# Nine gather buffers instead of six in the max-aggregation stage of a graph-network kernel

## The chip, the cores and the metric

One core of one Trainium2 chip. The metric is the device time of one execution in microseconds (us). Three executions of the kernel before took 3382.38, 3366.40 and 3394.16 us; the median, 3382.38, is the time before. The three lie within 0.8% of one another.

## The reference

A graph with 6250 nodes of 256 features and 100000 edges, sorted by destination. The features are normalised, clipped at zero, passed through four graph layers and added to the input:

```python
h = jnp.maximum(_layernorm(x, axis=-1), 0.0)
# layer 1: mean over the incoming edges
h = h @ W1_self + mean(h[src] by dst) @ W1_neigh + b1
# layer 2: maximum over the incoming edges
hp = relu(h @ W2_pool + b2_pool)
hmax = segment_max(hp[src], dst); hmax = where(deg > 0, hmax, 0)
h = h @ W2_self + hmax @ W2_neigh + b2
# layer 3: (sum over the incoming edges + h) / (deg + 1)
# layer 4: mean over the incoming edges, then the last dense layer
return x + h4 @ W_fc + b_fc
```

The change is in layer 2: for each of 100000 edges a row of 512 float32 numbers is fetched, and rows of one destination are reduced by maximum.

## The kernel before

Edges are put in six blocks of 52, 100, 220, 180, 130 and 100 steps (`BLOCKS`), 782 steps in all. In a block the 128 partitions hold 128 consecutive runs of edges, and step t of a partition is the t-th edge of its run. Layer 2 goes through the blocks from the last to the first.

One step is: GpSimd (POOL) issues an indirect DMA (line 1207) that gathers 128 rows of 2 KB, 256 KB in all, from `tab_p`, the table of `hp`, into one half of a buffer X of two rows per partition; VectorE (DVE) then takes the maximum with the row before it where both edges have the same destination (line 1212, one `scalar_tensor_tensor` over 128x512). The chain of maxima runs through all steps of a block. After each two steps one more DVE instruction (line 1246) folds the pair into one row, and SyncE (SP) issues a DMA that writes that row to `rows2` (line 1251). X may be filled again when this write has landed and the first maximum of the next pair, which reads X's second row as `prev`, has run.

X comes in turn from two pools of three buffers each: `xpool`, whose buffers also serve the prologue as scratch (line 478), and `xmore`, made at line 1028 for this stage. So a buffer is used again six pairs later, and at most twelve gathers are ahead of the oldest pair in use.

Between the steps the program places other work of this stage, a little at each step:

- `hub` (lines 317 to 341): one-hot tiles on ScalarE (ACT, lines 317 and 319) and DVE (`hm`, line 321), a matmul on TensorE (PE, line 327), copies on ACT, for adjacency blocks of later layers;
- `done2` (lines 1125 to 1161): for each of 49 node tiles one or two indirect gathers `tot` on POOL (line 1116), a load `th` on ACT's queue (line 1122), transposes and matmuls into `pm_prf` (lines 1135, 1140, 1143, 1146), then `prf` on DVE (line 1150), the split into three bf16 parts `r` (lines 294 to 297, ACT and DVE in turn), and a write to `tab_r` on SP (line 1156);
- `early` (line 1178): loads `ae` on SP, products `pd` on PE (line 460), sums `acc` on DVE (line 1008);
- `carry` at the end of a block: a gather `fixf` on POOL (line 1101) and its correction on DVE (line 1107);
- `node_rows`, 49-column arithmetic on DVE at the beginning of the stage (lines 926 to 993, `nr`).

Each engine works through its queue in order. The queues' order is set when the program is built, by the builder's idea of when things are ready, not strictly by the program text: lines 952 to 983 of `node_rows`, written for about steps 21 to 28, run in the trace at 1039 to 1131 us, when DVE is at about steps 50 to 100. Semaphores are placed by the builder too.

Of the kernel before, what the change touches and what calls it, by code (L numbers as in the profile page):

```python
# [9 lines left out]
F32 = mybir.dt.float32  # L10
# [10 lines left out]
P = 128  # L21
# [28 lines left out]
@with_exitstack  # L50
def kernel(ctx, tc, *aps):
    nc = tc.nc
    keep = ctx.enter_context(tc.tile_pool(name="keep", bufs=1))
    bad = keep.tile([P, 8], F32, name="bad")
    nc.vector.memset(bad, 0.0)
    flag = []

    def settle(fp, pp):

        worst = fp.tile([P, 1], F32, name="worst")  # L60
        nc.vector.tensor_reduce(worst, bad, AX.X, ALU.max)
        ones = fp.tile([P, P], F32, name="ones_f")
        nc.vector.memset(ones, 1.0)
        pw = pp.tile([P, 1], F32, name="pw_f")
        nc.tensor.matmul(pw, ones, worst, start=True, stop=True)
        odd = fp.tile([P, 1], F32, name="odd")
        nc.vector.tensor_scalar(odd, pw, 1.0, None, op0=ALU.min)
        oddI = fp.tile([P, 1], I32, name="oddI")
        nc.vector.tensor_copy(oddI, odd)
        flag.append(nc.values_load(oddI[:1, :1], min_val=0, max_val=1))  # L70

    fast_path(tc, bad, settle, *aps)
    general = flag[0]
    with tc.If(general > 0):
        general_path(tc, *aps)
# [3 lines left out]
def fast_path(  # L79
# [18 lines left out]
    FH = W1_self.shape[1]  # L98
# [129 lines left out]
    at = 0  # L228
# [76 lines left out]
    def build(d, A, keys, pool, psb, plain=True):  # L305
# [3 lines left out]
        for w in range(d * WT, (d + 1) * WT):  # L309
            hold = {}  # L310
            for k in range(k_of[w]):
# [12 lines left out]
                def run(k=k, w=w, hots=hots, hold=hold):  # L324
# [4 lines left out]
                    if k == k_of[w] - 1:  # L329
                        c = (w % WT) * WIN  # L330
                        if plain:
                            nc.vector.tensor_reduce(most[:, w : w + 1], hold[0], AX.X, ALU.max)
                        else:
# [52 lines left out]
    def sums(pool, psg, table, F, srcT, keyT, jb, h, done, deep, hub, wait=0, counts=0, todo=(), rest=0):  # L386
# [16 lines left out]
        def gather(j):  # L403
            nc.gpsimd.indirect_dma_start(  # L404
                out=ring[:, j % deep, :], out_offset=None, in_=table,
                in_offset=bass.IndirectOffsetOnAxis(ap=srcT[:, j - jb : j - jb + 1], axis=0),
            )
# [3 lines left out]
        for g in range(g_of[h][0], NG):  # L411
            pg = bank(psg, "pg", "pg", (F + counts,))
            n = min(G, T - g * G)
            for k in range(n):
                j = g * G + k
                X = ring[:, j % deep, :]
                gather(j)
                if j + ahead < T:
                    one_hot(j + ahead)
                for part in (2, 0, 1):  # L420
                    c = counts if part == 2 else 0
                    nc.tensor.matmul(  # L422
                        pg[:, : F + c], hot[j], X[:, part * F : (part + 1) * F + c],
                        start=(k == 0 and part == 2), stop=(k == n - 1 and part == 1),
# [44 lines left out]
    G2 = 2  # L469
    ahead = ctx.enter_context(tc.tile_pool(name="ahead", bufs=1))  # L470
    xpool = ctx.enter_context(tc.tile_pool(name="xrows", bufs=3))
# [19 lines left out]
    def segments():  # L491
# [15 lines left out]
        for b, tb in enumerate(BLOCKS):  # L507
# [6 lines left out]
                                    op0=ALU.is_equal)  # L514
            nc.vector.tensor_reduce(flen, eqf[:, sl_], AX.X, ALU.add)
            nc.vector.tensor_scalar(flen, flen, -1.0, None, op0=ALU.add)
# [31 lines left out]
    with ExitStack() as pro:  # L548
# [134 lines left out]
        def check_room():  # L683
# [15 lines left out]
            nc.vector.tensor_tensor(has, has, room, op=ALU.is_gt)  # L699
            nc.vector.tensor_reduce(bad[:1, 1:2], has, AX.X, ALU.max)  # L700

# [311 lines left out]
    with tc.tile_pool(name="fl2c", bufs=1) as ck, ExitStack() as late:  # L1013
# [11 lines left out]
        nc.scalar.dma_start(mkR, stash_k[:, 1, RB1:])  # L1025
        keepT = ck.tile([P, NB, P], F32, name="keepTf")
        contT = ck.tile([P, NB, P], F32, name="contTf")
        xmore = late.enter_context(tc.tile_pool(name="xrows2", bufs=3))

        def chains():  # L1030

# [93 lines left out]
        def done2(d):  # L1125
            tots, th = totals(d)
            for _ in range(4):
                yield
            hm = tots[0]
            for t in tots[1:]:  # L1130
                nc.vector.tensor_tensor(hm, hm, t, op=ALU.max)
            yield
            pt = bank(pst, "pt", "pt_hTf", (KH, P))
            for j in range(KH):
                nc.tensor.transpose(pt[:, j, :], hm[:, j * P : (j + 1) * P], ident)
            hT = wk.tile([P, KH, P], F32, name="hTf")
            nc.scalar.copy(hT, pt)
            pm = bank(psm, "pm", "pm_prf")
            for k in range(KI):
                nc.tensor.matmul(pm, th[:, k, :], usA[:, k, :], start=(k == 0), stop=False)  # L1140
            yield
            for k in range(KI):
                nc.tensor.matmul(pm, th[:, KI + k, :], usB[:, k, :], start=False, stop=False)
            yield
            for c in range(KH):
                nc.tensor.matmul(pm, hT[:, c, :], un[:, c, :], start=False, stop=(c == KH - 1))  # L1146
                if c == 1:
                    yield
            pr = wk.tile([P, FH], F32, name="prf")
            nc.vector.tensor_add(pr, pm, prow)  # L1150
            yield
            if d < H3:
                add3(d, pr)
            r3 = early_pool[0].tile([P, 3 * FH], BF16, name="r3", bufs=2 * BATCH + 1)
            parts(pr, FH, r3)
            nc.sync.dma_start(tab_r[d * P : (d + 1) * P, :], r3)
            if EARLY[0] <= d < EARLY[1]:
                ready.append((d, r3))
                if len(ready) == BATCH or d == EARLY[0]:
                    early_products()  # L1160
            yield
# [35 lines left out]
        at = 0  # L1197
        for b in reversed(range(NB)):
            tb = BLOCKS[b]
            t0 = offs[b] // P  # L1200
            prev = None
            for s0 in range(0, tb, G2):
                n = min(G2, tb - s0)
                X = (xmore if at // G2 % 2 else xpool).tile([P, G2, FH], F32, name="X2")
                for k in range(n):
                    t = t0 + s0 + k
                    nc.gpsimd.indirect_dma_start(  # L1207
                        out=X[:, k, :], out_offset=None, in_=tab_p,
                        in_offset=bass.IndirectOffsetOnAxis(ap=srcI[:, t : t + 1], axis=0),
                    )  # L1210
                    if s0 + k:
                        nc.vector.scalar_tensor_tensor(  # L1212
                            X[:, k, :], prev, same[:, t : t + 1], X[:, k, :],
                            op0=ALU.mult, op1=ALU.max,
                        )
                    prev = X[:, k, :]
                    at += 1
                    if at > 8:
                        next(steps, None)
                        if todo and next(todo[0], 0) == 0:  # L1220
                            todo.pop(0)
                    if at == MADE_AT:
                        for _ in steps:
                            pass
                        top.close()
                        early_pool.append(
                            top.enter_context(tc.tile_pool(name="early3", bufs=1)))
                    if at <= EARLY_AT:
                        hub.advance(math.ceil(len(first) * max(0, at - 16) / (EARLY_AT - 16)))
                    else:  # L1230
                        hub.advance(len(first) + math.ceil(
                            len(rest) * (at - EARLY_AT) / (T - 100 - EARLY_AT)))
                    early.advance(early.done + math.ceil(early.left() / 40))
                    if s0 + k > 2 and ends and next(ends[0], 0) == 0:
                        ends.pop(0)
                        tiles += [d for d in reversed(range(NT)) if b_of[d][0] == last_b]
                    if tiles and not ends and begun2 < NT * (at - FIRST_AT) / (T - 20 - FIRST_AT):
                        now.append(done2(tiles.pop(0)))
                        begun2 += 1
                    for g in list(now):  # L1240
                        if next(g, 0) == 0:
                            now.remove(g)
                r0 = s0 // 2
                if s0 + n < tb:
                    t = t0 + s0 + 1
                    nc.vector.scalar_tensor_tensor(  # L1246
                        X[:, 0, :], prev, same[:, t : t + 1], X[:, 0, :],
                        op0=ALU.mult, op1=ALU.max,
                    )
                    n = 1  # L1250
                nc.sync.dma_start(
                    runs[b][r0 * P : (r0 + n) * P, :].rearrange("(g p) f -> p g f", p=P),
                    X[:, :n, :],
                )
            end = carry(b, prev)
            next(end)
            ends.append(end)
            last_b = b
# [46 lines left out]
    with ExitStack() as on:  # L1305
# [8 lines left out]
        with tc.tile_pool(name="fl3", bufs=2) as wk:  # L1314
# [32 lines left out]
            late = ((EARLY[1], 44), (44, NT), (0, EARLY[0]))  # L1347
# [681 lines left out]
```

## Time and profile before

| What | us |
|---|---|
| median of three executions | 3382.38 |
| the profiled execution | 3393.26 |
| its span, first to last instruction | 3391.8 |
| prologue and layer 1, to the first gather of layer 2 | 0 to 957 |
| layer 2, first gather to the end of the last maximum | 957 to 2330.5 |
| layer 2's end: last carry, last node tile, first loads of layer 3 | 2330.5 to 2362 |
| layers 3 and 4 | 2362 to 3391.8 |

The profiled execution is 10.9 us (0.3%) above the median. Everything that the change touches lies in the 1373 us of the second stage. A view of that stage is read by engine: busy time is what the engine computes or issues; "idle before" is what it stood still, by what ended the wait. "issue" means that the wait was for nothing that the profile shows; "remote" stands for a release whose origin is not in the trace.

### The profile page before, as it was taken

The numbers are of one execution on the slowest core, as the hardware profiler recorded it, in microseconds if no ns is written. First come the engines' busy times: TensorE is split into PE (matmuls) and PEld (weight loads), VectorE is DVE, ScalarE is ACT, GpSimd is POOL, SyncE is SP. The second block draws the span as 40 slices with busy tenths as digits, with TensorE's granted clock in tenths as the row PEclk, the third lists the DMA queues.
The fourth block names the chain that finished last, engine by engine and source line by source line (L and its number), as shares of the span: only waits on it lengthen the run. The fifth ranks groups of instructions, "written<-read, shape, count | busy, mean of one in ns | idle before, by whom it ended". The sixth has DMA issues, their size and how long they took to land.

```text
span 3391.8 us, 42009 instructions
## 1 busy us (share of the span) xinstructions
PE 2546.3 (75%) x12637; PEld 1418.2 (42%) x12719; DVE 2109.1 (62%) x5394; ACT 987.3 (29%) x2703; POOL 2098.4 (62%) x2255
## 2 busy tenths in 40 slices
PE   4557788888867565586888864873888888788888
PEld 2134455555543222233333332431333333577776
DVE  7845555555358887787878786875456656333333
ACT  4745555554146777531301110000000001000000
POOL 4265565555556687776776666664566666566664
PEclk9678999999999677798899986985999999899999
DMA  5454555555578788898988888886999998766775
GB/s 173 152 142 137 158 165 168 162 169 169 170 247 267 260 281 264 282 303 272 297 295 279 270 292 265 271 262 202 344 328 340 350 331 306 242 198 199 200 204 167
DMA packets 354555, 812.52 MB, mean 240 GB/s; under 512 B 58078, under 2 KB 151494, under 8 KB 354284
## 3 DMA queue, kind: packets, MB, share of 16 engines
q0 software_dynamic: 146080, 513.65, 49.5%
q1 hardware_dynamic: 150152, 240.63, 19.6%
q10 hardware_dynamic: 58084, 55.44, 5.5%
q8 instruction: 103, 1.69, 0.2%
q14 instruction: 136, 1.11, 0.1%
HBM read 611.14 MB, written 199.17 MB: 239 GB/s over the span
## 4 chain that ended last, share of the span: by engine, by line
PE 46%; DMA 15%; issue 14%; DVE 13%; another core or an unknown queue 4%; POOL 3%; ACT 3%; SPq 0%; ACTq 0%; DVEq 0%; POOLq 0%
PE pd L460 19%; PE pg L422 12%; DVE X L1212 6%; DMA X<-rows,srcIf 5%; DMA ring<-tab_r,srcE 4%; PE pm_hp L896 3%; PE pb L327 3%; PE pm_hp L899 2%; POOL X L1207 2%; DVE X L1246 2%; PE pm_prf L1146 1%; DMA zt<-tab_r 1%; DMA rows<-X 1%; PE pm_w L261 1%
## 5 line engine op out<-in xcount | busy, mean ns | idle before, releaser
L1207 POOL DMA_INDIRECT X<-rows,srcIf x782 | 894.8, 1144 | 406.8 <-issue 195.2
L422 PE MATMUL pg<-ring,hot 128*128 128x256 bf16 (+2 forms) x3375 | 689.4, 315 | 132.6 <-DMA ring<-tab_r,srcE 47.4
L404 POOL DMA_INDIRECT ring<-tab_h,srcT x474 | 450.8, 951 | 330.0 <-issue 94.7
L460 PE MATMUL pd<-zt,ac 128*128 128x256 bf16 (+1 forms) x3442 | 584.4, 300 | 59.6 <-issue 41.8
L422 PEld LDWEIGHTS <-hot 128*128 128x128 bf16 x3390 | 337.9, 101 | 401.5 <-issue 246.1
L404 POOL DMA_INDIRECT ring<-tab_r,srcE x342 | 330.9, 967 | 203.5 <-PE pg L422 99.7
L460 PE MATMUL pd<-r,ae 128*128 128x512 bf16 x1493 | 376.0, 398 | 98.3 <-DVE acc L1008 49.1
L460 PEld LDWEIGHTS <-ac 128*128 128x128 fp8e4 x3462 | 338.2, 99 | 217.0 <-issue 91.8
L404 POOL DMA_INDIRECT ring<-tab_s,srcE x314 | 300.2, 956 | 192.5 <-PE pg L422 65.0
L441 DVE SCALAR_TENSOR_TENSOR acc<-pg,M,acc 128x259 f32<-128x259 f32 (+2 forms) x518 | 273.0, 560 | 234.5 <-PE pg L422 122.1
L327 PE MATMUL pb<-hm,hs 128*128 128x392 bf16 x781 | 260.7, 380 | 170.7 <-ACT A L337 64.1
L319 ACT ACTIVATE hs<-ht,onef 128x128 bf16<-128x128 bf16 x781 | 290.8, 398 | 299.8 <-PE pb L327 173.9
L1212 DVE SCALAR_TENSOR_TENSOR X<-X,samef 128x512 f32<-128x512 f32 x391 | 291.9, 747 | 67.4 <-DMA X<-rows,srcIf 48.1
L400 DVE TENSOR_SCALAR hot<-iota_bf,keyE 128x128 bf16<-128x128 bf16 x656 | 156.2, 268 | 279.2 <-PE pg L422 180.9
L1212 DVE SCALAR_TENSOR_TENSOR X<-X,samef,X 128x512 f32<-128x512 f32 x385 | 286.8, 745 | 33.7 <-DMA X<-rows,srcIf 25.8
L460 PEld LDWEIGHTS <-ae 128*128 128x128 fp8e4 x1536 | 155.9, 101 | 332.2 <-issue 191.5
L1246 DVE SCALAR_TENSOR_TENSOR X<-X,samef 128x512 f32<-128x512 f32 x385 | 287.2, 746 | 4.8 <-DVE nr L966 0.4
L400 DVE TENSOR_SCALAR hot<-iota_bf,keyT 128x128 bf16<-128x128 bf16 x474 | 119.6, 266 | 173.2 <-PE pg L422 65.8
L1146 PE MATMUL pm_prf<-unf,hTf 128*128 128x512 f32 x392 | 200.1, 645 | 17.3 <-issue 10.2
L460 PE MATMUL pd<-Z,A 128*128 128x256 bf16 (+1 forms) x1176 | 193.9, 281 | 6.4 <-issue 6.0
L327 PEld LDWEIGHTS <-hs 128*128 128x128 bf16 x781 | 81.1, 105 | 251.7 <-issue 140.1
L896 PE MATMUL pm_hp<-Wa,th 128*128 128x512 f32 x196 | 118.6, 736 | 83.6 <-ACT th L890 43.7
(314 smaller groups left out, 3076.5 us busy)
## 6 DMA issues: line engine op xcount, KB each, us to landing
rows<-X SPq DMA_DIRECT2D x385, 256.0 KB
tab_r<-r SPq DMA_DIRECT2D x49, 384.0 KB
tab_a<-A SPq DMA_DIRECT2D x18, 784.0 KB
tab_t<-th SPq DMA_DIRECT2D x49, 256.0 KB
rows<-hpf SPq DMA_DIRECT2D x49, 256.0 KB
th<-tab_t ACTq DMA_DIRECT2D x49, 256.0 KB
X<-rows,srcIf POOLq DMA_INDIRECT x782
ac<-tab_a ACTq DMA_DIRECT2D x108, 112.0 KB
```

The lines of the kernel that those rows point to most:

```text
L319: nc.scalar.activation(hots[0], t, AF.Relu, bias=one, scale=-1.0)
L327: nc.tensor.matmul(hold[0], hots[0], hots[1], start=(k == 0), stop=(k == k_of[w] - 1))
L400: nc.vector.tensor_scalar(hot[j], iota_b, keyT[:, j - jb : j - jb + 1], None, op0=ALU.is_equal)
L404: nc.gpsimd.indirect_dma_start(out=ring[:, j % deep, :], out_offset=None, in_=table, in_offset=bass.IndirectOffsetOnAxis(ap=srcT[:, j - jb ...
L422: nc.tensor.matmul(pg[:, : F + c], hot[j], X[:, part * F : (part + 1) * F + c], start=(k == 0 and part == 2), stop=(k == n - 1 and part == 1),
L441: nc.vector.scalar_tensor_tensor(acc[d], pg, m, acc[d], op0=ALU.mult, op1=ALU.add)
L460: nc.tensor.matmul(hold[0][:, : F + c], a, z[:, part * F : (part + 1) * F + c], start=(s == ss[0] and part == 2), stop=(s == ss[-1] and pa ...
L896: nc.tensor.matmul(ph, th[:, k, :], Wa[:, k, :], start=(k == 0), stop=False)
L1146: nc.tensor.matmul(pm, hT[:, c, :], un[:, c, :], start=False, stop=(c == KH - 1))
L1207: nc.gpsimd.indirect_dma_start(out=X[:, k, :], out_offset=None, in_=tab_p, in_offset=bass.IndirectOffsetOnAxis(ap=srcI[:, t : t + 1], axis=0),
L1212: nc.vector.scalar_tensor_tensor(X[:, k, :], prev, same[:, t : t + 1], X[:, k, :], op0=ALU.mult, op1=ALU.max,)
L1246: nc.vector.scalar_tensor_tensor(X[:, 0, :], prev, same[:, t : t + 1], X[:, 0, :], op0=ALU.mult, op1=ALU.max,)
```

## The change

The second pool gets six buffers, and the choice goes round nine: pairs 0, 3 and 6 of each nine take one of `xpool`'s three, the others one of `xmore`'s six.

```diff
-        xmore = late.enter_context(tc.tile_pool(name="xrows2", bufs=3))
+        xmore = late.enter_context(tc.tile_pool(name="xrows2", bufs=6))
...
-                X = (xmore if at // G2 % 2 else xpool).tile([P, G2, FH], F32, name="X2")
+                X = (xpool if at // G2 % 9 in (0, 3, 6) else xmore).tile(
+                    [P, G2, FH], F32, name="X2")
```

`at` counts steps over all blocks, `G2` is 2. A buffer has 2 x 512 x 4 = 4096 bytes per partition, so the stage holds 12 KB more, and the pools that are made after `xmore` (`fl2`, and `fw2`, later `early3` in its place) lie 12 KB higher.

## The prediction

> **What bounds the kernel now.** I read the table of costliest groups first, because it names the gather as the largest POOL group and the maxima as the largest DVE work:
>
> ```profile
> L1207 POOL DMA_INDIRECT X<-rows,srcIf x782 | 894.8, 1144 | 406.8 <-issue 195.2 <-DVE X L1212 47.5 <-DVE X L1246 39.3
> L1212 DVE SCALAR_TENSOR_TENSOR X<-X,samef 128x512 f32<-128x512 f32 x391 | 291.9, 747 | 67.4 <-DMA X<-rows,srcIf 48.1 <-issue 12.4 <-DVE X L1212 1.3
> ```
>
> 782 gathers keep POOL busy 894.8 us, and it is idle 406.8 us before them. Next the busy times of layer 2 alone, from its first gather to its last maximum:
>
> ```profile
> core 0: us, PE busy (x) PEld busy (x) DVE busy (x) ACT busy (x) POOL busy (x), PEclk, DMA share, GB/s
> 957.00:2330.00 1373.00, 960.64 (x3149) 434.86 (x3192) 1091.26 (x2061) 468.59 (x1332) 968.08 (x843) 0.83 0.86 278
> ```
>
> No engine is full: DVE 1091/1373 = 79%, POOL 968/1373 = 71%, PE 70%, DMA 0.86. The stage is a chain of queues that stop each other. So I turn to who waits for whom in the same window, POOL first:
>
> ```profile
> engine line waited for: us in total, times, longest us
> POOL X L1207 <- issue: 195.2, 623, 1.5
> POOL X L1207 <- DVE X L1212: 47.5, 37, 6.5
> POOL X L1207 <- DVE X L1246: 39.3, 35, 5.3
> POOL X L1207 <- DMA rows<-hpf: 33.2, 1, 33.2
> ...
> POOL X L1207 <- DVE hm L321: 19.6, 17, 6.0
> POOL X L1207 <- DMA rows<-X: 19.6, 26, 6.7
> ```
>
> then DVE:
>
> ```profile
> DVE X L1212 <- DMA X<-rows,srcIf: 73.9, 61, 5.9
> DVE acc L1008 <- remote: 47.7, 12, 7.5
> DVE prf L1150 <- remote: 31.5, 5, 8.1
> DVE X L1212 <- issue: 19.9, 27, 4.4
> ```
>
> and last one place in order of time, DVE's rows and then POOL's:
>
> ```profile
> 1878.47 0.75 DVE L1212 SCALAR_TENSOR_TENSOR X<-X,samef,X 128x512 f32<-128x512 f32 x1
> 1885.69 0.69 DVE L1008 TENSOR_TENSOR acc<-acc,pd 128x512 f32<-128x512 f32 x1 [6.47 <-remote]
> ```
>
> ```profile
> 1882.57 0.94 POOL L1207 DMA_INDIRECT X<-rows,srcIf  x1 [0.30 <-issue]
> 1889.07 1.50 POOL L1207 DMA_INDIRECT X<-rows,srcIf  x1 [5.55 <-DVE X L1212]
> 1892.11 1.17 POOL L1207 DMA_INDIRECT X<-rows,srcIf  x1 [1.54 <-issue]
> ```
>
> The reader should see a stop travelling: DVE stands 6.47 us before `acc`, whose matmuls on PE are late; the maxima queued behind it do not run, no buffer comes free, and POOL stands 5.55 us once its twelve gathers are out. When DVE goes on it uses up the gathers in store, and a little later waits for gathers that POOL could not issue. Such waits of POOL stand, nearly all, before the first gather of a pair, where the buffer is taken.
>
> **What the change removes.** Of POOL's 406.8 us idle I take off the 195.2 at "issue" (623 gaps of about 0.30 between two issues) and the 33.2 before the first gather (the end of layer 1). That leaves 178 us in some 150 gaps; each would keep its 0.30, so 178 - 45 = about 133 us are waits for a buffer. On the other side DVE waits 73.9 + 19.9 = 94 us for gathers. These 94 are all that faster gathers can give back directly.
>
> How much of it? Six more gathers in store are 6 x (1.25 to 1.44), about 8.1 us of POOL work (0.95 at the least and 1.14 in the mean, and the 0.30 gap). That covers the longest of POOL's waits (6.7). I went through the stage in order of time, added up POOL's waits for buffers, at most 8.1 us at a time, and let each later wait of DVE for a gather be paid from that: 63 of the 94 us are paid. The others follow no wait of POOL (the first gathers after 957, and gathers that took long by themselves). So 63 us is the gain if nothing else stops DVE instead.
>
> Something will. DVE's other waits in this window, for PE, ACT, `tot` and `fixf`, are about 170 us (`acc` 47.7 + 10.9 + 4.7, `prf` 31.5 + 11.1 + 4.6 + 3.6, `fixf` 14.0, `hm` 14.0 + 3.4 + 2.4, `tot` 12.1, `r` and `prf` behind ACT 9.2). Between 1460 and 2020 us PE is busy 455 of 560, 81%. A maximum that comes earlier brings DVE earlier to an `acc` whose matmuls are no earlier. I let a third of the 63 come back as waits for PE: **gain 42 us**. Below, the gain is bounded by nothing at all, above by the 94.
>
> **A rule against the change.** The Trainium skill, "DMA: Bandwidth & Descriptors", section "Anatomy of one DMA — SWDGE (gpsimd) path", fits a DMA's time as 2.0 us plus the bytes at 436 GB/s: 2.6 us for 256 KB. The chain of waits shows more in this stage:
>
> ```profile
> 1261.29 5.28 DMA X<-rows,srcIf
> ...
> 1364.53 3.77 DMA rows<-X
> ```
>
> A buffer's round trip is two issues (2.5), the gather, three DVE instructions (3 x 0.75 = 2.2) and the write. With the rule's 2.6 for both transfers this is 9.9 us; six buffers last 6 x 1373/391 = 21.1 us, and the 11 us left would cover the longest stop of DVE (8.1): the gain would be nil. With the rows it is 2.5 + 5.3 + 2.2 + 3.8 = 13.8, 7.3 us are left, and stops of 6 to 8 us come through, as POOL's waits show. With nine buffers (31.6 us) 17.8 are left. I go by the rows.
>
> **What it adds and moves.** No instruction is added. Costs:
> - The pools after `xmore` lie 12 KB higher, over other tiles of layer 1. The first gather waits for the last `rows<-hpf` in any case (33.2 us, until 956.7), and by then layer 1's tiles are read. `wfcf`, loaded from 956.2 on, may start some us later; what it feeds is finished by about 1093, and the first matmul that needs it is at 1144. Zero, hidden by 50 us; without that cover at most its wait, a few us.
> - Layer 3's first tiles lie over these pools too, but they wait for the last `tab_r` write at 2358, 28 us after the last maximum. Zero. If that tail were gone, their load would wait for the last write of X (3.8 us).
> - `tot` and `fixf` stand in POOL's queue among the gathers. `fixf` reads what the last maxima of a block write, so POOL must let its store run down there, five times within the stage; a deeper store is no use at these places. No loss, as the gathers behind it wait now too.
> - The builder will order the queues anew, since buffers come free elsewhere. No row shows what that gives. Sideways moves of either sign are possible: PE is stopped 49.1 us by `acc` and 25.0 by `hm`, both set by where DVE's instructions stand among the maxima. I take zero, and half of their 74 us to either side as bounds.
>
> Sum: 0 to -94, with +-37 for the order; value taken -42. On the profiled execution 3393.3 - 42 = 3351; on the median 3382.4 - 42 = **3340 us**.
>
> **The rivals.**
> 1. *PE takes over* (0.17). All 63 us come back as waits for `pd` and `pm_prf`. For it: PE at 81% for 560 us, and its in-order lumps of 10 us (2170.5: 43 matmuls of `pd` in 12.2 us). Against it: PE itself stands 49 us for `acc` on DVE, and between 1140 and 1460 it is busy only 196 of 320. Time: 3382 +- 20.
> 2. *Slower: the extra gathers delay the small loads that PE waits for* (0.22). `th` (49 loads) and `ae` (128) run on other queues. The same page of the skill, section "Issuing engines are not separate DMA queues", says that all of them interleave on the same 16 DMA engines. `th` takes 5.6, 5.5 and 4.5 us where the chain of waits shows it, and PE waits 17.4 us for it, in 6 cases. When DVE stops, POOL will now send up to six gathers more, 1.57 MB, 5.7 us at 278 GB/s, beside them. Against it: DMA is at 0.86, not full, and loads are issued several steps ahead. Point of decision: 42 / 177 = 0.24 us of exposed delay per load undoes the gain; at twice that, 0.5 us, the loads cost 88 us, and the end is 3382 - 42 + 88 = 3428. A new queue order that puts `acc` and `hm` worse would add its part here.
> 3. *The whole bound* (0.07): all waits of DVE for gathers go and PE's stops shrink with them: 3382 - 85 = 3297.
> 4. *It doesn't do what it says.* If the two pools did not come round evenly, the shorter would decide. They do: three of nine pairs with three buffers, six of nine with six, both come round after nine pairs, and every block has an even number of steps. No chance is set aside.
>
> **How the numbers follow.** The forecast case (-15 to -65, value -42) has 0.54. A run of three executions spread over 0.8%, so about 1%, 34 us, is what can be told from no change. Of the forecast case 0.37 lies beyond -34 and 0.17 within; rival 3 adds 0.07 to faster; rival 1 is 0.17 of same; rival 2 gives 0.20 slower and 0.02 same. Faster 0.44, same 0.36, slower 0.20. The range runs from 3292 (just past rival 3) to 3428 (rival 2's value); what lies outside is the worse half of rival 2 and little else. The forecast case alone: 3317 to 3367.
>
> **What would show it.** Right: idle time before the gathers at line 1207, without "issue" and the first wait, falls from 178 to under 90; DVE's waits for gathers from 94 to about 40; the time from the first gather to the last maximum from 1373 to about 1330; outside that stage nothing moves by more than a few us. Rival 1: POOL's waits fall as said, and DVE's waits for `acc` and `prf` (114 us together) rise by as much. Rival 2: `th` and `ae` appear in PE's waits with more than 60 us, and the DMA share rises to 0.9. The prediction is wrong if POOL's waits fall and the stage is not shorter, or if they do not fall.

## The result, and the profile after

The kernel with nine buffers is slower: 3400.1 us against 3366.4 (medians of 20 executions each), ratio 1.0099 with a 95% interval of 1.0075 to 1.0123. With twenty executions the kernel before has a median of 3366.4 us, where the first three had 3382.4. My forecast was 3340. The profiled execution has a span of 3408.8 us, 17 more than that of before, where the medians are 34 apart: layer 2 is 28 longer, and what runs ahead of it, which the change does not touch, is 9 shorter.

The group table of the kernel after comes first (columns as before: busy us, mean ns of one, idle us before it):

```profile
L1208 POOL DMA_INDIRECT X<-rows,srcIf x782 | 924.5, 1182 | 402.3 <-issue 189.9 <-DVE X L1213 55.6 <-DMA rows<-hpf 32.3
...
L1213 DVE SCALAR_TENSOR_TENSOR X<-X,samef 128x512 f32<-128x512 f32 x391 | 291.1, 746 | 54.8 <-DMA X<-rows,srcIf 33.0 <-issue 17.1 <-DVE nr L976 0.5
```

Then layer 2 alone, from the first gather to the last maximum, by busy time of each engine:

```profile
core 0: us, PE busy (x) PEld busy (x) DVE busy (x) ACT busy (x) POOL busy (x), PEclk, DMA share, GB/s
948.00:2350.00 1402.00, 965.34 (x3151) 438.31 (x3195) 1087.67 (x2062) 468.25 (x1332) 987.90 (x843) 0.83 0.84 272
```

and who waited for whom in that window, POOL's rows and then DVE's (us in total, times, longest):

```profile
POOL X L1208 <- issue: 189.9, 612, 1.9
POOL X L1208 <- DVE X L1213: 55.6, 25, 6.4
POOL X L1208 <- DMA rows<-hpf: 32.3, 1, 32.3
POOL X L1208 <- DVE X L1247: 29.0, 29, 4.5
POOL X L1208 <- DVE hm L321: 23.4, 21, 7.2
```

```profile
DVE acc L1008 <- remote: 62.8, 17, 12.6
DVE X L1213 <- DMA X<-rows,srcIf: 50.0, 29, 5.9
DVE prf L1150 <- remote: 29.1, 5, 11.2
DVE tot L1131 <- DMA tot<-rows,rows_of: 21.0, 3, 11.4
DVE X L1213 <- issue: 19.4, 9, 8.3
DVE fixf L1107 <- DMA fixf<-rows,fixIf: 17.9, 2, 10.3
```

The stage takes 1402 us instead of 1373. DVE computes as long as before (1088 against 1091 us), so it stands longer. Its waits for gathers fell only from 94 to 69 us, and its other waits grew by more: `acc` from 47.7 to 62.8, `tot` and `fixf` from 26 to 39 in these rows. POOL's idle time without "issue" and the first wait is 402.3 - 189.9 - 32.3 = 180 us, as before (178). Yet the store is fuller: when POOL issues a row gather, 9.5 rows issued earlier have no finished maximum yet, in the mean of all gathers; before the change it was 5.0.

One block border shows how the order of POOL's queue changed. The last maximum of the second block ends at 1379 us. These are the last of POOL's rows from there to `fixf`, in order of time:

```profile
1392.42 1.25 POOL L1208 DMA_INDIRECT X<-rows,srcIf  x1 [0.30 <-issue]
1393.97 7.52 POOL L1208 DMA_INDIRECT X<-rows,srcIf  x1 [0.30 <-DVE hm L321]
1401.80 0.94 POOL L1208 DMA_INDIRECT X<-rows,srcIf  x1 [0.30 <-issue]
1403.04 0.94 POOL L1208 DMA_INDIRECT X<-rows,srcIf  x1 [0.30 <-issue]
1404.29 0.94 POOL L1101 DMA_INDIRECT fixf<-rows,fixIf  x1 [0.30 <-issue]
```

and DVE's:

```profile
1400.36 0.31 DVE L321 TENSOR_SCALAR hm<-iota_w,mkR 128x392 bf16<-128x392 f16 x1
1408.30 0.69 DVE L1107 TENSOR_TENSOR fixf<-fixf,pcf 128x512 f32<-128x512 f32 x1 [7.62 <-DMA fixf<-rows,fixIf]
```

In the kernel before, the same border's last maximum ends at 1373, and POOL's next rows end with

```profile
1382.12 1.25 POOL L1207 DMA_INDIRECT X<-rows,srcIf  x1 [0.30 <-issue]
1383.68 1.25 POOL L1101 DMA_INDIRECT fixf<-rows,fixIf  x1 [0.30 <-DMA rows<-X]
```

and DVE does not stand before the correction:

```profile
1394.97 0.68 DVE L1107 TENSOR_TENSOR fixf<-fixf,pcf 128x512 f32<-128x512 f32 x1
```

There `fixf` issues 10.7 us after the last maximum. After the change it stands behind six more row gathers, one of which took 7.52 us, and issues 25.0 us after the last maximum. DVE, with its rows in store, has run through its maxima by then and stands 7.6 us. The builder made this order, by its own idea of when buffers come free. In the traces, `fixf` of the first five borders stands behind 118, 246, 432, 652 and 750 row gathers instead of 112, 240, 422, 642 and 744; `tot` gathers stand 8 row gathers later in the mean; and on DVE 5 more maxima stand ahead of an `acc` addition. Whether this order costs the time is a question for the experiments; it turns out below that the later `fixf` and `tot` do not explain it.

### The profile page after: what moved, and what is told of

It reads as the page before. It is cut to its first block, busy times and chain, and to the rows that moved or that the text cites. A ratio compares the mean times of both kernels' runs of the same rounds, so it can differ in the third digit from the quotient of the medians.

```text
span 3408.8 us, 41968 instructions
## 1 busy us (share of the span) xinstructions
PE 2543.7 (75%) x12637; PEld 1421.2 (42%) x12719; DVE 2105.3 (62%) x5394; ACT 986.3 (29%) x2703; POOL 2118.2 (62%) x2255
## 4 chain that ended last, share of the span: by engine, by line
PE 45%; DMA 16%; issue 14%; DVE 13%; another core or an unknown queue 5%; POOL 3%; ACT 3%; ACTq 0%; SPq 0%; POOLq 0%; DVEq 0%
PE pd L460 18%; PE pg L422 12%; DMA X<-rows,srcIf 7%; DVE X L1213 5%; DMA ring<-tab_r,srcE 4%; PE pm_hp L896 3%; PE pb L327 3%; PE pm_hp L899 2%; PE pm_prf L1146 2%; POOL X L1208 2%; PE pm_w L261 2%; DVE X L1247 2%; DMA zt<-tab_r 1%; PE pm_prf L1140 1%
## 5 line engine op out<-in xcount | busy, mean ns | idle before, releaser
L1208 POOL DMA_INDIRECT X<-rows,srcIf x782 | 924.5, 1182 | 402.3 <-issue 189.9
L321 DVE TENSOR_SCALAR hm<-iota_w,mk 128x392 bf16<-128x392 f16 x461 | 151.0, 342 | 47.8 <-PE pb L327 23.1
```

The lines of the kernel that those rows point to most:

```text
L321: nc.vector.tensor_scalar(hots[1], iota_w, mk[:, r : r + 1], None, op0=ALU.is_equal)
L1208: nc.gpsimd.indirect_dma_start(out=X[:, k, :], out_offset=None, in_=tab_p, in_offset=bass.IndirectOffsetOnAxis(ap=srcI[:, t : t + 1], axis=0),
```

## The experiments

Three theories: *placement* (12 KB shift), *sequence* (the builder's new queues; the expectations also say *order*), *depth* (gathers further ahead at run time). Ratios are to the kernel before, run in the same set on the same chip; brackets are 95% intervals.

### Sequence and depth apart

A kernel can be held to another kernel's queues. Both builds number their instructions alike, so a list of numbers from one can be replayed in the other as edges of order without a wait:

```diff
-    fast_path(tc, bad, settle, *aps)
+    fast_path(tc, bad, settle, *aps); replay(tc)
...
+    at = {i.name: i for i in tc.nc.cur_bb.bb.instructions}
...
+        for a, b in zip(names, names[1:]):
+            tc.add_manual_dep(at[b], a, mybir.DependencyInfo(
+                mybir.DependencyClass.NoSync, mybir.DependencyReason.DATA), reason="replay")
```

Placement has an edit of its own:

```diff
-        xmore = late.enter_context(tc.tile_pool(name="xrows2", bufs=3))
+        xmore = late.enter_context(tc.tile_pool(name="xrows2", bufs=3)); pad = late.enter_context(tc.tile_pool(name="pad", bufs=1)).tile([P, 3, G2, FH], F32, name="pad"); nc.gpsimd.memset(pad[:, 0, 0, 0:1], 0.0)
```

> Nine buffers as in the kernel after, but every engine's queue of layer 2 and of what follows is held to the sequence that the kernel before had (the row gathers among themselves kept in program order, which moves 28 places on POOL). Theory 'order' (the loss comes from the new sequence: fixf and tot gathers behind more row gathers on POOL, row maxima ahead of the acc and prf additions on DVE): the 34 us are gone, ratio to before 0.990 to 1.002. Theory 'depth' (up to eighteen gathers under way instead of twelve make other loads and gathers late, whatever the sequence): still 1.007 to 1.012. Theory 'placement' (the three tiles move fl2, fw2 and early3 by 12 KB): also still 1.007 to 1.012.

> Nine buffers, with POOL's queue alone held to the sequence of before (the fixf gathers 2.5 steps behind their place instead of 8.8, the tot gathers as early as before); the other engines are sequenced anew. 'Order', if its POOL half carries the loss: 0.992 to 1.004, and the waits for tot and fixf on DVE fall back from 45 us to about 26. 'Order', if its DVE half carries it (maxima ahead of acc and prf, PE waiting for pd): 1.006 to 1.012, with PE's pd wait still above 60 us. 'Depth' and 'placement': 1.007 to 1.012.

> Nine buffers, with DVE's queue alone held to the sequence of before (maxima 4.3 steps behind acc's place instead of 0.5 ahead); POOL's fixf gathers stay at 7.8 steps behind their place, tot at 26 ahead instead of 32. 'Order', DVE half: 0.992 to 1.004 and PE's pd wait back from 67 to about 49 us. 'Order', POOL half: 1.006 to 1.012, the waits for tot and fixf on DVE at 45 us or more. 'Depth' and 'placement': 1.007 to 1.012.

> Six buffers and the kernel before's sequence, with 12 KB that nothing uses put where the three added tiles lie, so that fl2, fw2 and early3 stand at the addresses of the kernel after. 'Placement': 1.007 to 1.012. 'Order' and 'depth': 0.998 to 1.002.

A second set on a like chip gave the controls:

> The control for the first run: six buffers, and exactly the sequence that nine_old_order had on all five engines (that of before, the row gathers on POOL in program order, 28 places moved). The two kernels differ in nothing but the number of buffers that the gathers may fill. 'Depth' (more gathers under way cost the other half of the loss): 0.998 to 1.002 here, against 1.0051 with nine. 'The 28 places' (seven gathers that before issued ahead of their turn are worth it): 1.004 to 1.007 here too.

> The sequence without the buffers: six buffers, with DVE, PE, ACT and SP held to the sequence of the kernel after (row maxima and run stores among themselves in program order, 81 places on DVE and 27 on SP), POOL's queue as it comes out beside them. 'Order': slower than before, 1.004 to 1.02 (maxima ahead of acc and prf, and with fewer gathers in store the wait for a gather on DVE rises above the 97 us of before). If only the buffers cost: 0.998 to 1.003.

> Nine buffers, with DVE, PE, ACT and SP held to the sequence of before and POOL's queue free to take the new room (fixf gathers 7.8 steps behind their place, tot 26 ahead, as with DVE alone held). If POOL's sequence carries part of the loss: above nine_old_order's 1.0051, 1.007 to 1.010, with more waiting for tot and fixf than its 30 us. If the sequence of DVE is what counts: 1.003 to 1.007, as for DVE alone held (1.0057).

> The kernel after with its own sequence, but row gathers, maxima and run stores each in program order among themselves (42 places on POOL, 81 on DVE, 27 on SP): what the crossings at the block borders are worth. If nothing: 1.008 to 1.012, like after. If crossing costs (maxima of the next block ahead of this block's last ones delay the chain tot, fixf): 0.998 to 1.006. If it helps: 1.013 to 1.02.

| Kernel | buffers | queues held to those of before | ratio |
|---|---|---|---|
| six_pad | 6 | (its own are the same) | 1.0002 [0.9981, 1.0024] |
| six_sorted_all | 6 | all, gathers in program order | 1.0013 [0.9994, 1.0033] |
| six_new_nopool | 6 | none: DVE, PE, ACT, SP as after, maxima and stores in program order | 1.0013 [0.9989, 1.0036] |
| nine_old_order | 9 | all, gathers in program order | 1.0051 [1.0029, 1.0073] |
| nine_old_dve | 9 | DVE | 1.0057 [1.0033, 1.0080] |
| nine_old_nopool | 9 | all but POOL | 1.0082 [1.0056, 1.0107] |
| nine_old_pool | 9 | POOL | 1.0206 [1.0177, 1.0235] |
| nine_new_sorted | 9 | none: as after, gathers, maxima, stores in program order | 1.0038 [1.0020, 1.0057] |
| the kernel after | 9 | none | 1.0099 [1.0075, 1.0123] |

What follows:
- Placement costs nothing that can be told (1.0002).
- With six buffers the new sequence of four engines costs nothing that can be told. So my first theory, that the new order of DVE and PE is the loss, falls for six buffers.
- Depth costs by itself: nine_old_order and six_sorted_all have one and the same sequence, 1.0051 against 1.0013. They ran in two sets; a pair in one set follows below. Neither theory had its number there, since the loss is split.
- Putting gathers, maxima and stores each into program order, so that no next-block row crosses the end of a block, takes 0.6% off the kernel after (1.0099 to 1.0038). Why crossing costs is not shown. It is not by the later `fixf` and `tot`: nine_new_sorted has them behind as many row gathers as the kernel after, and DVE waits 42 us for them (45 after, 26 before), yet it loses no more than nine_old_order, which has them at their old places (30 us).
- A mixture of two sequences can be worse than either: with POOL on the old queue and DVE on the new one, DVE waits 144 us for gathers (97 before). That POOL serves `tot` early while DVE asks for rows early is my reading, not tested. No theory had 1.0206 in its range; nine_old_dve, too, lies between the ranges named for it.

### A set on which PE hardly stops

The third set was meant to measure what a store that is never empty can give, and to look for a better kernel. In ideal_store the gathers go to tiles that nobody reads:

```diff
+                        out=Z[:, k, :], out_offset=None, in_=tab_p,
...
+                    if len(done) >= 12: tc.add_manual_dep(g.ins, done[-12], mybir.DependencyInfo(
+                        mybir.DependencyClass.Sync, mybir.DependencyReason.DATA), reason="pace")
...
-                            X[:, k, :], prev, same[:, t : t + 1], X[:, k, :],
+                            X[:, k, :], prev, same[:, t : t + 1], held,
```

and in late6_six and late10_nine the transposes of the block's last row are traced later (late6_six is shown; the other has nine buffers and a 10 for the 6):

```diff
-            next(end)
...
-                    if s0 + k > 2 and ends and next(ends[0], 0) == 0:
+                    if s0 + k > 6 and ends and next(ends[0], 0) == 0:
```

> The ceiling of any deeper store: the sequence of before (row gathers, maxima and stores in program order), but the 782 row gathers write tiles that nobody reads, held to at most twelve rows ahead of the maxima, and the maxima take a constant row in their place. Left out: the use of the gathered rows; the gathers, their transfers, all maxima and stores stay. DVE so never waits for a row gather. My prediction's own step (two thirds of DVE's gather waits come back as time): 0.975 to 0.985, DVE's 89 to 97 us of waits gone and no others grown. 'Lockstep' (DVE and PE wait for each other through two-bank PSUM rings, so that DVE arrives earlier only to wait for PE): 0.993 to 1.003, with the waits for acc, prf and hm grown by most of the 90 us.

> The control for the run with unread gathers: six buffers with exactly its sequence, gathers read as in before (against the kernel before, 28 places moved on POOL, 39 on DVE, 14 on SP). All theories: 0.998 to 1.004.

> A look for a version that beats both: PE stands up to 38 us at each block's end at the transposes of the block's last row (114 us in four stops in before). Here carry's first part is traced seven steps into the next block instead of at once, six buffers, queues as the builder then orders them. 'Lockstep': PE has other work in those stops and DVE is served earlier, 0.98 to 0.995. If PE's stop is cover that costs nothing (DVE has its maxima meanwhile): 0.997 to 1.005. If the fix-up is then late and fixf and tot gathers with it: above 1.005.

> The same with nine buffers and eleven steps: the last row's tile is held longer, which six buffers can afford less. 'Lockstep': 0.98 to 0.997. Otherwise 1.005 to 1.015 like the kernel after.

| Kernel | ratio |
|---|---|
| ideal_store | 1.0048 [1.0030, 1.0066] |
| six_old_sorted | 0.9973 [0.9959, 0.9987] |
| late6_six | 1.0001 [0.9990, 1.0013] |
| late10_nine | 0.9981 [0.9970, 0.9992] |

The two kernels with the later transposes do no better than six_old_sorted: late6_six lies in the range named for stops of PE that cost nothing, late10_nine between its two ranges. The whole set is faster: the kernel before takes 2989.6 us there, 3362 and 3360 in the two sets ahead. One group of layers 3 and 4 shows the difference, first in six_sorted_all of the second set:

```profile
L460 PE MATMUL pd<-zt,ac 128*128 128x256 bf16 (+1 forms) x3442 | 583.9, 300 | 61.1 <-issue 43.5 <-DMA ac<-tab_a 10.6 <-DMA zt<-tab_r 3.9
```

then in six_old_sorted of the third, nearly the same program:

```profile
L460 PE MATMUL pd<-zt,ac 128*128 128x256 bf16 (+1 forms) x3462 | 567.8, 299 | 20.0 <-DMA ac<-tab_a 11.9 <-DMA zt<-tab_r 4.3 <-DMA zt<-tab_s 3.8
```

The matmuls are as fast; the 43.5 us of "issue" are gone. Over the whole span PE stands 248 us so, in 243 stops, on the one chip, and 9 us in 3 stops on the other. The traces of before and after and of the first two sets have 212 to 277 us. I call this a chip *with stops* or *without*. The record gives the chip of the first and of the third set the same number, 2, and does not name the machine, so whether it was another chip or the same one in another state is open.

Nothing in a trace says what the stops are. The granted clock does not tell: in the trace of before it is at half, some 4 us later, in all 13 unexplained stops of over 3 us, but also in 44 of the 49 waits of that length whose cause is named. It goes down after PE has stood, mostly whatever the reason. So a stop may cost more than its own length: the clock is at half for 735 us of six_sorted_all and for 535 us of six_old_sorted. Some waits of a known kind may be counted among the stops: the longest, 24.4 us in six_new_nopool, ends 0.15 us after the last maximum of a block, for which PE's transposes wait.

ideal_store asks the main question, against its control of the same sequence, six_old_sorted. Its DVE never waits for a row gather, where the control waits 119 us, and yet it is slower, 1.0048 against 0.9973. DVE's longest waits in layer 2, first of the control, then of ideal_store:

```profile
DVE X L1212 <- DMA X<-rows,srcIf: 114.3, 132, 4.1
DVE tot L1131 <- DMA tot<-rows,rows_of: 23.4, 6, 5.4
```

```profile
DVE fixf L1107 <- DMA fixf<-rows,fixIf: 123.8, 3, 61.3
DVE tot L1131 <- DMA tot<-rows,rows_of: 31.6, 5, 16.1
```

DVE outruns POOL, and then stands up to 61 us for a `fixf` gather that is queued behind POOL's own row gathers. The control's waits at `fixf` and `tot` are 9 and 23 us. The stage's 842 gathers at 1.15 us, with 0.30 us between two, are 1221 of the control's 1272 us: POOL is nearly full there, and no number of buffers makes it issue faster. So on this chip taking away all of DVE's gather waits gave nothing. It is no bound for every kernel with nine buffers, though: its stage took 1300 us, and that of nine_pace8 below takes 1267.

### The same kernels on both kinds of chip

> The kernel after, unchanged, beside the three others on whatever chip this is. 'Stops' (the loss needs PE's unexplained stops): on a chip with the stops 1.007 to 1.012 as before; on a chip without them 0.985 to 0.999, because DVE there waits 119 us for row gathers and hardly for PE. 'Sequence' (the order of the queues costs on any chip): 1.004 to 1.012 on both.

> Nine buffers with carry's first part traced eleven steps into the next block; 0.9981 on the chip without the stops. 'Stops': with the stops 1.003 to 1.012, without them again 0.997 to 0.999. If tracing carry later is what helped: below 1.000 on both.

> Nine buffers with exactly the sequence of six_old_sorted (that of before, row gathers, maxima and stores in program order). 'Depth costs by itself': ratio to six_old_sorted 1.002 to 1.005 on either chip. 'Stops': with the stops 1.002 to 1.005, without them 0.985 to 0.999.

> The pair's other half, six buffers: 0.9973 on the chip without the stops. There again 0.996 to 0.999; on a chip with the stops 0.998 to 1.003, as six_sorted_all (1.0013).

This set fell on a chip with stops (before: 3318.4 us), the last one on a chip without (2991.4). Its new kernel, nine_pace8, is nine_old_sorted with

```diff
+                    if len(done) >= 8: tc.add_manual_dep(g.ins, done[-8], mybir.DependencyInfo(mybir.DependencyClass.Sync, mybir.DependencyReason.DATA), reason="pace")
```

after each row gather `g`; `done` holds the maxima.

> nine_old_sorted (nine buffers, 1.0077 on a chip with stops) with one wait added: a row gather may not issue before the maximum eight rows earlier is done. Nothing is left out, and the sequence is the same. 'Gathers ahead prolong PE's stops': on a chip with stops 0.996 to 1.003, and no joint stop of PE and DVE ahead of an acc or prf addition above 7 us (16 us before). 'The buffers cost in another way': 1.006 to 1.012, or more by the added wait. On a chip without stops: 1.000 to 1.012, since DVE's waits for gathers grow and nothing shrinks.

> The kernel after, unchanged, beside it. On a chip with stops 1.008 to 1.013 for the third time. On a chip without them: 'stops' 0.985 to 1.001, 'sequence' (fixf and tot gathers behind more row gathers on POOL, the crossings at the block borders) 1.003 to 1.01.

| Kernel | with stops | without |
|---|---|---|
| the kernel after | 1.0120 [1.0092, 1.0147] | 1.0013 [0.9996, 1.0030] |
| late10_nine | 1.0114 [1.0073, 1.0154] | 0.9981 [0.9970, 0.9992] |
| nine_old_sorted | 1.0077 [1.0046, 1.0109] | not run |
| six_old_sorted | 0.9997 [0.9970, 1.0023] | 0.9973 [0.9959, 0.9987] |
| nine_pace8 | not run | 0.9933 [0.9913, 0.9953] |

The two nine-buffer kernels that ran on both lose 1.1 and 1.3 points more with stops; the six-buffer one 0.2. The pair of one sequence in one set, nine_old_sorted and six_old_sorted, puts depth alone at 1.0077/0.9997 = 0.8% on a chip with stops, more than the 0.2 to 0.5% I expected. The first two sets put it at 0.4%. Both figures are uncertain by 0.3 to 0.4 points, and with the 0.6% for crossing they add up to about the loss of 1.0 to 1.2% at the lower figure only; so the split is known roughly.

The pair shows depth alone in DVE's waits, first with six buffers, then with nine:

```profile
DVE X L1212 <- DMA X<-rows,srcIf: 73.7, 81, 3.5
DVE acc L1008 <- remote: 48.1, 16, 7.4
```

```profile
DVE acc L1008 <- remote: 75.0, 12, 17.0
DVE X L1213 <- DMA X<-rows,srcIf: 38.7, 40, 4.1
...
DVE prf L1150 <- remote: 21.1, 4, 11.3
```

Over all releasers DVE's gather waits fall from 91 to 53 us, and its waits for `acc` and `prf`, which take PE's products, rise from 78 to 114. All its waits apart from gathers rise from 134 to 195, and the stage from 1329 to 1349.

How depth and stops may meet, the longest stop of nine_old_sorted shows, in order of time (nine of the rows left out are gathers of POOL):

```profile
1737.41 0.75 DVE L1213 SCALAR_TENSOR_TENSOR X<-X,samef 128x512 f32<-128x512 f32 x1
1737.84 1.15 POOL L1208 DMA_INDIRECT X<-rows,srcIf  x1 [0.30 <-issue]
1739.29 0.95 POOL L1208 DMA_INDIRECT X<-rows,srcIf  x1 [0.30 <-issue]
...
1751.79 0.95 POOL L1208 DMA_INDIRECT X<-rows,srcIf  x1 [0.30 <-issue]
1753.04 0.95 POOL L1208 DMA_INDIRECT X<-rows,srcIf  x1 [0.30 <-issue]
1755.16 0.32 SPq L1178 DMA_DIRECT2D ae<-tab_a  x1
1755.17 0.69 DVE L1008 TENSOR_TENSOR acc<-acc,pd 128x512 f32<-128x512 f32 x1 [17.01 <-remote]
...
1755.91 2.72 PE L460 MATMUL pd<-r,ae 128*128 128x512 bf16 x6 [16.70 <-issue]
```

PE stands for nothing that the trace names, DVE stands before an `acc` whose release has no origin in the trace, and POOL issues twelve gathers in a row. Two microseconds after the last of them ends, PE goes on. No load of instructions falls into this stop. With six buffers POOL runs out of room sooner. Stops of PE and DVE together of over 3 us in layer 2 (this takes in those at `tot` and `fixf`) sum to 35 to 81 us in the five traces with six buffers from chips with stops, with none over 8.9 us. In the nine traces with nine buffers they sum to 76 to 130 us, and eight of these have stops of 9 us and more, up to 16.8.

That the gathers *prolong* PE's stop is not shown. nine_pace8, made to test it, met a chip without stops. And two things limit what these sums show. PE's unexplained stops in layer 2 alone sum to 73 to 109 us with six buffers (the 24.4 us left out) and to 94 to 125 with nine, which overlap. And the two nine-buffer kernels on a chip without stops that are not held to eight rows, late10_nine and after_third, have 78 and 72 us of such joint stops too, up to 13.7. Why depth costs time on a chip with stops stays open.

On the chip without stops nine_pace8 is the fastest of all, and faster than both kernels; I had expected 1.000 to 1.012. DVE's waits in layer 2 there, first of after_third, then of nine_pace8:

```profile
DVE X L1213 <- DMA X<-rows,srcIf: 93.5, 77, 8.6
DVE tot L1131 <- DMA tot<-rows,rows_of: 40.0, 7, 12.5
DVE fixf L1107 <- DMA fixf<-rows,fixIf: 24.8, 3, 11.3
```

```profile
DVE X L1214 <- DMA X<-rows,srcIf: 109.3, 130, 3.8
DVE tot L1131 <- DMA tot<-rows,rows_of: 32.4, 6, 7.5
```

Held to eight rows ahead and to the old sequence, DVE waits for gathers often but never long, and for `tot` and `fixf` 33 us in all, as in six_old_sorted (32). How much of this is the wait and how much the old sequence is not known: nine_old_sorted did not run on a chip without stops, nor six buffers with the same wait anywhere. Where the 0.4% against six_old_sorted (another set) comes from, I did not find: their stages are 1267 and 1272 us.

## Why the prediction was wrong

- *"I let a third of the 63 come back as waits for PE."* This step failed, and it turned the sign: 21 us were to come back, and more than all did. DVE's waits outside the gathers grew by 58 us in the profiled execution (175 to 234, gaps over 0.15 us), where its gather waits fell by 26 (97 to 71 in the same count). Most of the growth is for `tot` (15), `acc` (11), `fixf` (4) and `rl` (line 1039, from under 1 to 18). With the sequence held, in the pair of nine_old_sorted and six_old_sorted, they grew by 60 us against 38 saved, 36 of it for `acc` and `prf`. Why they grew by more than was saved stays open. Rival 1 was nearer than the forecast, but its sign, `acc` and `prf` up by as much as was saved, shows in the pair only: in the kernel after they went from 114 to 124.
- *"63 us is the gain if nothing else stops DVE instead."* This term was too large. DVE's gather waits fell to 69 us, not to about 40; in the pair they fell by 38. POOL's idle time did not fall at all, where I had named under 90; in the pair it fell from 141 to 119. I took POOL's 133 us of buffer waits as time in which it could have worked for DVE. On a chip without stops there was no such time: its issue fills 1221 of 1272 us, and ideal_store, with every gather wait gone, was not faster. On the chip of the forecast the same 1221 us leave 150 of 1373, so there POOL's rate alone does not rule out 42 us.
- *"No loss"* for `tot` and `fixf`. Wrong as to the waits: the builder put more row gathers ahead of them on POOL. DVE's waits for both, summed over all releasers, went from 26 to 45 us, and on a chip without stops from 32 (six_old_sorted) to 57 (after_third), which is the whole difference of the two stages' DVE waits there (170 and 191, with 6 less for gathers). With stops, nine_new_sorted pays nearly the same waits (42) without the loss of the kernel after.
- *"The builder will order the queues anew ... I take zero."* The bound of 37 us held, the centre did not: the order of the rows among themselves, with next-block rows across a block's end, costs 0.6%, 20 us. Of the 74 us of PE's waits that I named for it, those for `acc` rose from 49 to 67 and those for `hm` stayed at 25.
- *The rule.* I set the Trainium skill's 2.6 us ("DMA: Bandwidth & Descriptors", the SWDGE section) aside for rows of 5.28 and 3.77 us. Those rows came from the chain of waits, which picks the late ones. Counted by the queue's packets, a gather's last packet has ended 3.1 us after POOL's instruction, in the mean, and 3.2 after the change: nearer to the rule. With the rule the gain was nil, which is nearer to the result, though not for its reason, since DVE did wait 94 us for gathers with six buffers. I also put 2.6 us on the write, which that section does not cover: it is about DMAs that GpSimd issues, and the write is issued by SP.
- *Rival 2* had the right sign by the wrong way. PE waits 11.0 us for `th` (17.4 before), the DMA share is 0.84, and the gathers under way when POOL starts one are 2.3 in the mean with six and with nine buffers alike: the added buffers hold rows that have landed. Its trigger, POOL sending more while DVE stands, is in the stop shown above; that PE itself would stand meanwhile was not in it.
- *Placement, "zero"*, was right (1.0002), and after the stage little moved (1061 and 1059 us). The range held the time by the width that Rival 2 gave it, not by its way; the direction was wrong.

## What to carry to other kernels

Before deepening a store, ask whether the producer could fill it: multiply its issues by their time and set that beside the stage, or build the kernel whose consumer never waits. Then count what the consumer waits for besides: here these waits grew by more than the store saved. In this kernel a change of buffer counts re-sequenced the queues of every engine looked at, so replay the old sequence before judging the depth. And in an in-order queue, what stands behind the bulk work (here two small kinds of gathers) waits longer when more of the bulk is put ahead of it; bounding how far the bulk runs is worth a try, but what the bound alone gives was not separated here.

## What the hardware showed that I had not expected

A gather's issue on POOL depends on DVE. In all traces it takes 0.95 us (median) where DVE is busy under a tenth of it, and 1.14 to 1.22 in the mean where DVE is busy over nine tenths; single ones take up to 15 us. Of the 18 gathers over 2 us in layer 2 of the profiled execution of after, 11 end 0.81 to 0.83 us after a pause of DVE begins, like the 7.52 us above; before, 11 of 18 do. 15 of the 18 ran beside `hm`'s `tensor_scalar` (line 321), and 16 of 18 before. The Trainium skill, "SBUF — State Buffer", section "Who interferes with whom", states that a `tensor_scalar` can enter a two-port mode, and that whichever of DVE and GpSimd then has the shared port pair blocks the other for its whole instruction. That fits in kind, but not in length: one `hm` takes 0.32 us, and all 18 ran beside maxima as well, two of them (5.35 and 6.86 us) beside maxima without any `hm`. Which instructions hold POOL was not tested.

The time beyond 1.15 us of the gathers over 2 us is 46 us before, 75, 64 and 60 in the three traces of after, and 100 in ideal_store against 41 in its control. So where DVE never waits for rows, the engine that fetches them is slowed. Depth alone does not do this: with the sequence held it is 47 us with six buffers and 46 with nine, and 41 and 36 in the other pair.

And the sets differ in PE's unexplained stops, 181 to 277 us against 2 to 10. With them the kernel before took 3318 to 3366 us, without them 2990, and the change cost 1.0 to 1.2% with them and nothing that can be told without. The stops are shorter than that difference, and what else differs between the sets was not found, apart from the time at half clock that goes with them.
